# A mixture-of-experts and attention kernel: gathering results row by row instead of block by block

## The chip, the cores and the metric

The kernel runs on one core of a Trainium2 chip. Its engines work side by side, each on its own queue of instructions: TensorE (PE) multiplies matrices, VectorE (DVE) and ScalarE (ACT) work on rows, GpSimd (POOL) copies and issues indirect DMAs, and SyncE (SP) issues most of the plain DMAs. The metric is the device time of one execution in microseconds (us). Before the change it is 738.46 us, the median of three runs between 733.2 and 739.15.

## What is computed

The input is 4,096 tokens of 128 numbers (16 sequences of 256). Each passes a mixture-of-experts layer, an attention layer, and the same mixture-of-experts layer again, each added to the residual.

```python
x = x + 0.5 * _L0_ffn_ref(_layernorm(x, axis=-1), ...)
x = x + _L0_attn_ref(_layernorm(x, axis=-1), ...)
x = x + 0.5 * _L0_ffn_ref(_layernorm(x, axis=-1), ...)
```

The part that matters here is the expert layer. Every token chooses 4 of 32 experts, and its result is the sum of the four experts' outputs, each with the token's weight for that expert:

```python
vals, idx = jax.lax.top_k(gf, K)               # K = 4 of E = 32
w = jax.nn.softmax(vals, axis=-1)
combine = jnp.zeros((T, E)).at[jnp.arange(T)[:, None], idx].add(w)
h1 = jnp.einsum('th,efh->tef', tf, w1) + b1
hw = _swiglu(h1) * combine[:, :, None]
out = jnp.einsum('tef,ehf->th', hw, w2) + combine @ b2
return x + out.reshape(B, S, H)
```

The matmuls with data and weights are in float32; counts and masks are in bfloat16, where they are exact.

## The kernel before, in words

**Tiles.** The 4,096 tokens are 8 blocks of 512; four blocks form a group, so there are two groups (`n_grp` = 2, `GB` = 4). A block is held as 4 tiles of 128 tokens (`NJ` = 4). There are four expert runs: the first layer for groups 0 and 1 (`first[0]`, `first[1]`), and the last layer for groups 0 and 1 (`last[0]`, `last[1]`).

**To the experts.** `route` computes the gate, finds the top four experts of each token, the mask `m` (token chose expert), the weights `comb`, and each token's `rank` within its expert and tile. `dispatch` then finds where every expert's rows lie in the sorted order of the whole group. Tokens are sorted with matmuls against one-hot matrices (L677) into small blocks of five rows (`RB` = 5), all of one expert, and each tile's 128 such blocks are scattered with one indirect DMA (L596) into the DRAM buffer `xs[g]`. A block of five rows of 128 numbers is 2,560 B.

**The experts.** `experts` walks over 23 steps (`NQS`). In each it loads four tiles of 125 sorted rows, has POOL copy the four experts' first weights into a buffer (L717, five buffers), multiplies (L737), applies the activation on ACT and DVE (L741, L742, L747), multiplies again (L755), and writes the result rows to `ys[g]` in DRAM.

**Back from the experts.** `combined` undoes the sorting for one block of 512 tokens. For each tile of 128 tokens it gathers the same 128 small blocks with one indirect DMA (L786) from `ys[g]`, so four gathers per block. Then DVE builds a matrix `u` that holds, for each of the five rows of a small block, which token it belongs to and with which weight (L809, ten instructions per block), from two products `pa` and `pw` (L798 to L800); and PE multiplies it with the gathered rows (L816: 4 tiles x 5 rows, and each f32 matmul is two passes). The bias of the second expert weights is one more matmul per tile (L819), and the residual is added last (L822). The gathered tiles `gt` live in four buffers.

**What runs beside what.** `groups` strings the four expert runs together. Beside each run of experts, a generator of other work is advanced a few steps (`beside`) after every expert step:

- experts of `first[0]`, beside `enter(1)`: routing and dispatch of group 1
- experts of `first[1]`, beside `middle(0)`: for each block of group 0, `combined`, `attention` and `route` for the last layer, then `dispatch`
- experts of `last[0]`, beside `middle(1)`: the same for group 1
- experts of `last[1]`, beside `leave(0)`: `combined` of group 0, and the output is written
- after that, `leave(1)` alone: `combined` of group 1, and the output is written

`staggered` keeps up to three blocks of `middle` in flight, a new one after nine steps. The program text gives the order of priority; each engine's queue is laid out when the program is built, and an instruction that is ready early may be placed ahead, as the trace shows for small memsets. On the chip each queue then runs in its order.

Of the kernel before, what the change touches and what calls it, by code (L numbers as in the profile page):

```python
# [10 lines left out]
F32 = mybir.dt.float32  # L11
BF16 = mybir.dt.bfloat16
U32 = mybir.dt.uint32
I32 = mybir.dt.int32
AF = mybir.ActivationFunctionType
ALU = mybir.AluOpType
AX = mybir.AxisListType
# [5 lines left out]
P = 128  # L23
NJ = 4
TB = NJ * P
SEQ = 2
GB = 4
GJ = GB * NJ
NE = 32
TOPK = 4  # L30
# [6 lines left out]
RB = 5  # L37
# [7 lines left out]
NQ = NT // NJ  # L45
NQS = 23
NB = NT * BT
LIMIT = 7.0
ALPHA = 1.702
EPS = 1e-5  # L50
SILU_LIMIT = ALPHA * LIMIT / (1.0 + math.exp(-ALPHA * LIMIT))
NONE = -1.0e38
ROUND = 8388608.0


@with_exitstack
def kernel(
# [22 lines left out]
    nc = tc.nc  # L80
# [8 lines left out]
    const = ctx.enter_context(tc.tile_pool(name="const", bufs=1))  # L89
    wpool = ctx.enter_context(tc.tile_pool(name="weights", bufs=1))  # L90
    grp = ctx.enter_context(tc.tile_pool(name="grp", bufs=2))
# [108 lines left out]
    place_f = const.tile([P, FREE], F32, tag="place_f", name="place_f")  # L200
    nc.vector.tensor_scalar(place_f, step_f, self_f, None, ALU.add)

    ones = const.tile([P, P], BF16, tag="ones", name="ones")
    nc.gpsimd.memset(ones, 1.0)

# [76 lines left out]
    def bank(name):  # L282
        pool, tag = banks[0]
        banks.rotate(-1)
        return pool.tile([P, TB], F32, tag=tag, name=name)
# [115 lines left out]
    class Group:  # L401


        def __init__(self, g, name):
            self.g, self.name = g, name
            self.blocks = []
            self.n = grp.tile([P, GB], BF16, tag="n", name=f"n_{name}", bufs=3)
            self.row = grp.tile([P, 2, GJ], U32, tag="row", name=f"row_{name}", bufs=3)

        def held(self, b, tag, shape, dtype, bufs):  # L410
# [3 lines left out]
        def enter(self, b):  # L414
            self.blocks.append(Block())
            self.held(b, "tn", [P, NJ, P], F32, GB + 1)
            self.blocks[b].xr = dram.tile(
                [P, NJ * P], F32, tag=f"xr_{self.name}{b}", name=f"xr_{self.name}{b}"
            )

            self.held(b, "rank", [P, P], BF16, 2 * GB + 2)
            self.held(b, "combT", [P, P], F32, 2 * GB + 2)
            return self.blocks[b]

        def sort(self, b):
            self.held(b, "seg", [P, P], F32, 2 * GB + 2)
            self.held(b, "seg_b", [P, P], BF16, 2 * GB + 2)
            self.held(b, "off", [P, P], BF16, 2 * GB + 2)
            return self.blocks[b]

    def split(src, dtype, engine, tag, name, bufs=1):
# [12 lines left out]
    def route(st, src, b, co):  # L444

        name = f"{st.name}{b}"
        k = st.enter(b)
# [27 lines left out]
        for j in range(NJ):  # L475
            nc.vector.match_replace(left[:, j, :], v8[:, j, :], g[:, j, :], 2.0 * NONE)
        m = small.tile([P, NJ, NE], BF16, tag="m", name=f"m_{name}")
        nc.vector.tensor_tensor(m, left[:, :, 0:NE], g[:, :, 0:NE], ALU.not_equal)
        comb = small.tile([P, NJ, NE], F32, tag="comb", name=f"comb_{name}")
        nc.vector.tensor_tensor(  # L480
            comb, g[:, :, 0:NE], v8[:, :, 0:1].to_broadcast([P, NJ, NE]), ALU.subtract
        )
# [4 lines left out]
        nc.tensor.matmul(  # L487
            prank[:, 0 : 2 * P], m.rearrange("p j e -> p (j e)"),
            upto_self.rearrange("p c t -> p (c t)"), start=True, stop=True,
        )  # L490

        n = small.tile([P, 1], F32, tag="n32", name=f"n32_{name}")
# [33 lines left out]
    def dispatch(st, clear=False):  # L526
# [36 lines left out]
        for c in range(2):  # L563
# [6 lines left out]
        nc.vector.scalar_tensor_tensor(  # L570
            at, f[:, 0:1].to_broadcast([P, GB]), float(BT), at, ALU.mult, ALU.add
        )
        pick = small.tile([P, GB, 2 * NJ], F32, tag="pick", name=f"pick_{name}")
        nc.vector.tensor_copy(pick[:, :, NJ:], own.unsqueeze(1).to_broadcast([P, GB, NJ]))
        nc.vector.tensor_tensor(
# [81 lines left out]
        for b in range(GB):  # L657
# [8 lines left out]
            for t in range(NJ):  # L666
# [20 lines left out]
                    nxt = tables(b + 1)  # L687
                yield
        scattered[name] = sc

    def loaded(tab, q, engine, top):
        _, vals = nc.values_load_multi_w_load_instructions(
# [81 lines left out]
    def combined(st, b, tag):  # L774
# [45 lines left out]
                yield  # L820
        r = tmp.tile([P, NJ, P], F32, tag=tag, name=f"{tag}_{name}", bufs=3)
        nc.vector.tensor_tensor(r, pu, xr, ALU.add)  # L822
        yield r

    def logits(hT, w, name):
# [137 lines left out]
    def routes(g, gap, most):  # L963
        srcs = []
        for b in range(GB):
            if g * GB + b not in x_tiles:
                load_x(g * GB + b)
            srcs.append(x_tiles.pop(g * GB + b))
        co = coefficients(srcs, first[g].name)
        yield  # L970

        def block(b):
            yield from route(first[g], srcs[b], b, co[:, :, b * NJ : (b + 1) * NJ])

        yield from staggered((block(b) for b in range(GB)), gap, most)

    def enter(g, clear):
        first[g] = Group(g, f"{run_name}f{g}")
        yield from routes(g, 2, 2)
        yield from dispatch(first[g], clear)  # L980

    def middle(g):
        last[g] = Group(g, f"{run_name}l{g}")

        def block(b):
            for x1 in combined(first[g], b, "x1"):
                yield
            for x2 in attention(x1, f"{run_name}{g}{b}"):
                yield
            yield from route(last[g], x2, b, coefficients([x2], f"{last[g].name}{b}"))  # L990

        yield from staggered((block(b) for b in range(GB)), 9, 3, True)
        yield from dispatch(last[g])

    def leave(g):
        def block(b):
            for y in combined(last[g], b, "x1"):
                yield
            nc.sync.dma_start(
                out_blk[g * GB + b], y.rearrange("p (i s) h -> p i (s h)", i=SEQ)  # L1000
            )
            yield

        yield from staggered((block(b) for b in range(GB)), 3)
# [141 lines left out]
```

## Time and profile before

| | |
|---|---|
| median of three runs | 738.46 us |
| the profiled execution | 734.1 us |
| its span, first to last instruction | 732.0 us |
| busy: PE, PE weight loads | 620.1 us (85%), 574.3 us (78%) |
| busy: DVE, ACT, POOL | 483.1 us (66%), 379.5 us (52%), 284.5 us (39%) |
| mean granted TensorE clock | 0.938 |
| gathers L786, scatters L596 | 64 and 73 indirect DMAs |

Busy time is the time in which an engine executes; the rest is waiting. PE's busy time is not PE at its peak, since matmuls overlap. A share of the whole span is a mean over stages that have different limits, so the stages have to be read one by one. Instructions that only issue or wait are not counted as busy.

### The profile page before, as it was taken

Reading aid. Unit: us, or ns where it says so; the run is one execution under the profiler, and the core shown is the slowest. Engines: PE = TensorE matmul, PEld = TensorE weight load, DVE = VectorE, ACT = ScalarE, POOL = GpSimd, SP = SyncE. Lnnn points to the kernel's source line nnn. Section 1 sums busy time; section 2 is a strip of 40 time slices with the busy share of each in tenths; the row PEclk is TensorE's granted clock in tenths of the full one; section 3 lists DMA queues with packets and bytes.
Section 4 is the critical chain, followed back from the end, with each engine's and each line's share of the span. In section 5 each row is a group of like instructions: output and inputs, shape, how many; then the busy total and the mean of one; then the engine's idle time right before and its main releaser. Section 6 shows DMA issues by size and latency. Waiting matters only on the chain.

```text
span 732.0 us, 15990 instructions
## 1 busy us (share of the span) xinstructions
PE 620.1 (85%) x4897; PEld 574.3 (78%) x4897; DVE 483.1 (66%) x1823; ACT 379.5 (52%) x902; POOL 284.5 (39%) x567
## 2 busy tenths in 40 slices
PE   3677489979978988988997998988889789999595
PEld 1466389878978977977896887877789689999585
DVE  6863975855555688887774469888878535554443
ACT  2753376735543766864552455775655335445210
POOL 3023424467645422122365532402227645434242
PEclk9887779999999999998999999999999989999989
DMA  7999346477656435124355644513434667765463
GB/s 229 374 336 328 138 139 172 128 259 227 193 157 198 128 90 140 48 81 128 112 197 194 185 119 124 143 44 85 129 100 174 215 182 213 199 189 160 111 204 118
DMA packets 132695, 122.45 MB, mean 167 GB/s; under 512 B 9626, under 2 KB 118714, under 8 KB 132602
## 3 DMA queue, kind: packets, MB, share of 16 engines
q1 hardware_dynamic: 117658, 71.62, 34.6%
q0 software_dynamic: 10960, 44.90, 18.2%
q10 hardware_dynamic: 3984, 4.82, 1.8%
q8 instruction: 43, 0.70, 0.4%
q14 instruction: 50, 0.41, 0.2%
HBM read 57.78 MB, written 63.52 MB: 166 GB/s over the span
## 4 chain that ended last, share of the span: by engine, by line
PE 53%; DVE 21%; DMA 11%; ACT 7%; issue 6%; POOL 1%; another core or an unknown queue 0%; SPq 0%; POOLq 0%; ACTq 0%; DVEq 0%
PE ph_l L737 8%; PE ph_f L737 7%; PE p_l L677 4%; PE pu_f L816 4%; PE po_l L755 4%; PE po_f L755 4%; PE p_f L677 3%; PE pu_l L816 3%; DMA xs<-s_f,row_f 3%; PE pxT_l L723 2%; DMA gt_l<-ys,row_l 2%; DMA xq_l<-xs 1%; DMA w_sb<-in_w_dram 1%; PE pxT_f L723 1%; DVE lin_f L742 1%
## 5 line engine op out<-in xcount | busy, mean ns | idle before, releaser
L717 POOL COPY w_l<-w_sb 128x256 f32 x184 | 71.3, 416 | 124.4 <-PE ph_l L737 118.6
L717 POOL COPY w_f<-w_sb 128x256 f32 x184 | 70.3, 414 | 117.7 <-PE ph_f L737 116.2
L737 PE MATMUL ph_f<-xT_f,w_f 128*128 128x125 f32 x736 | 97.7, 281 | 1.4 <-DVE lin_f L742 1.1
L737 PE MATMUL ph_l<-xT_l,w_l 128*128 128x125 f32 x736 | 95.5, 279 | 0.1
L737 PEld LDWEIGHTS ph_f<-xT_f,w_f 128*128 128x128 f32 x736 | 90.9, 197 | 2.4 <-POOL w_f L717 1.4
L737 PEld LDWEIGHTS ph_l<-xT_l,w_l 128*128 128x128 f32 x736 | 89.6, 196 | 0.6 <-issue 0.3
L742 DVE TENSOR_SCALAR lin_l<-ph_l 128x250 f32<-128x250 f32 x92 | 37.8, 413 | 53.8 <-ACT a_l L741 53.3
L742 DVE TENSOR_SCALAR lin_f<-ph_f 128x250 f32<-128x250 f32 x92 | 37.5, 412 | 37.3 <-ACT a_f L741 36.2
L816 PE MATMUL pu_l<-gt_l,u_l 128*128 128x128 f32 x320 | 46.2, 290 | 11.5 <-DMA gt_l<-ys,row_l 7.5
L816 PEld LDWEIGHTS pu_l<-gt_l,u_l 128*128 128x128 f32 x320 | 42.7, 203 | 16.8 <-issue 9.8
L677 PE MATMUL p_f<-tn_f,o_f 128*128 128x128 f32 x320 | 46.3, 303 | 10.2 <-DVE rank_f L438 4.1
L677 PEld LDWEIGHTS p_f<-tn_f,o_f 128*128 128x128 f32 x320 | 43.1, 214 | 14.1 <-DVE rank_f L438 4.2
L816 PE MATMUL pu_f<-gt_f,u_f 128*128 128x128 f32 x320 | 45.7, 284 | 7.3 <-DMA gt_f<-ys,row_f 5.6
L755 PE MATMUL po_f<-w_sb,a_f 128*125 x368 | 49.9, 278 | 1.3 <-DVE a_f L747 0.9
L755 PE MATMUL po_l<-w_sb,a_l 128*125 x368 | 49.3, 277 | 1.4 <-DVE a_l L747 0.8
L741 ACT ACTIVATE a_l<-ph_l 128x250 f32<-128x250 f32 x92 | 34.7, 379 | 29.2 <-PE ph_l L737 25.1
L596 POOL DMA_INDIRECT xs<-s_f,row_f x32 | 31.3, 977 | 45.4 <-ACT s_f L682 23.4
L786 POOL DMA_INDIRECT gt_l<-ys,row_l x32 | 30.6, 958 | 44.2 <-PE pu_l L816 23.6
L816 PEld LDWEIGHTS pu_f<-gt_f,u_f 128*128 128x128 f32 x320 | 40.3, 194 | 9.3 <-DMA gt_f<-ys,row_f 5.2
L741 ACT ACTIVATE a_f<-ph_f 128x250 f32<-128x250 f32 x92 | 34.5, 381 | 23.8 <-PE ph_f L737 18.7
L755 PEld LDWEIGHTS po_f<-w_sb,a_f 128*125 128x125 f32 x368 | 45.0, 191 | 1.7 <-ACT yq_f L760 1.0
L755 PEld LDWEIGHTS po_l<-w_sb,a_l 128*125 128x125 f32 x368 | 44.9, 191 | 1.6 <-ACT yq_l L760 1.0
(339 smaller groups left out, 1456.9 us busy)
## 6 DMA issues: line engine op xcount, KB each, us to landing
xq_f<-xs SPq DMA_DIRECT2D x46, 224.0 KB
ys<-yq_f SPq DMA_DIRECT2D x46, 224.0 KB
xq_l<-xs SPq DMA_DIRECT2D x46, 224.0 KB
ys<-yq_l SPq DMA_DIRECT2D x46, 224.0 KB
xs<-zero SPq DMA_DIRECT2D x14, 500.0 KB
w_sb<-in_w_dram SPq DMA_DIRECT2D x4, 1024.0 KB
ys<-zero SPq DMA_DIRECT2D x2, 1250.0 KB
x<-in_x_dram SPq DMA_DIRECT2D x8, 256.0 KB
```

What stands on the lines that cost most here:

```text
L596: ins = nc.gpsimd.indirect_dma_start(out=xs[st.g][:, :], out_offset=bass.IndirectOffsetOnAxis(ap=index, axis=0), in_=rows.rearrange("p r h ...
L677: nc.tensor.matmul(p0[:, r, :] if r < 4 else p1[:, 0:P], o[:, r, :], k.tn[:, t, :], start=True, stop=True,)
L717: nc.gpsimd.tensor_copy(w[:, s, :], w_flat[:, bass.ds(at[2 * c + s], 2 * P)])
L723: nc.tensor.transpose(pt[:, t, 0:RT], xq[:, t, :], ident[:RT, :RT])
L737: nc.tensor.matmul(ph[:, part, s, 0:RT], w_q[c][:, s, part * P : (part + 1) * P], x_q[:, 2 * c + s, :], start=True, stop=True,)
L741: nc.scalar.activation(a[:, ts, :], ph[:, 0, :, 0:RT], AF.Silu, scale=ALPHA)
L742: nc.vector.tensor_scalar(lin[:, ts, :], ph[:, 1, :, 0:RT], LIMIT + 1.0, 1.0 - LIMIT, ALU.min, ALU.max,)
L755: nc.tensor.matmul(po[:RT, t, :], hT[:, t, :], w_flat[:, bass.ds(at[t] + 2 * P, P)], start=True, stop=True,)
L786: nc.gpsimd.indirect_dma_start(out=gt.rearrange("p r h -> p (r h)"), out_offset=None, in_=ys[st.g][:, :], in_offset=bass.IndirectOffsetOnA ...
L816: nc.tensor.matmul(pu[:, t, :], u[:, r, s, :], got[t][:, r, :], start=(r == 0), stop=False)
```

## The change

Three of the four combines now use a new function, `gathered`, in the place of `combined`; only `leave(1)`, the last phase, keeps `combined`. `gathered` reads each token's four result rows (512 B each) directly: 16 indirect DMAs per block, one for each tile and each of the four choices, and DVE multiplies each row with the token's weight and adds it, 16 instructions per block. The bias matmul and the residual stay. The matrix `u` and its products go.

For this the kernel has to know each token's four row numbers and weights in the order of tokens, not in the sorted order. `route` makes a second rank product, with tokens on the partitions, and keeps it with the mask in `rk` (a chosen expert is marked by the large constant `CHOSEN`); it keeps the weights in `cw`. The new generator `places` adds each expert's place in the sorted order, and takes the four largest entries of each token with DVE's maximum instruction; these are the row numbers `row_k`. A comparison with all 32 entries picks the weights `w_k`. `mixed` interleaves `places` with the other generators, every fourth step beside `enter(1)` and every sixth beside `middle`. The numbers of buffers of `rank`, `combT`, `seg`, `seg_b` and `off` shrink, since most of them aren't needed again later.

```diff
+I16 = mybir.dt.int16
+assert NB * RB < 16384
+CHOSEN = 16384.0
...
+    ones_f = const.tile([P, P], F32, tag="ones_f", name="ones_f")
+    nc.gpsimd.memset(ones_f, 1.0)
...
+            self.rk = grp.tile([P, GB, P], I16, tag="rk", name=f"rk_{name}")
+            self.cw = grp.tile([P, GB, NJ, NE], F32, tag="cw", name=f"cw_{name}")
...
-            self.held(b, "rank", [P, P], BF16, 2 * GB + 2)
-            self.held(b, "combT", [P, P], F32, 2 * GB + 2)
+            self.held(b, "rank", [P, P], BF16, GB + 1)
+            self.held(b, "combT", [P, P], F32, 2 * GB + 1)
...
-            self.held(b, "seg", [P, P], F32, 2 * GB + 2)
-            self.held(b, "seg_b", [P, P], BF16, 2 * GB + 2)
-            self.held(b, "off", [P, P], BF16, 2 * GB + 2)
+            self.held(b, "seg", [P, P], F32, GB + 1)
+            self.held(b, "seg_b", [P, P], BF16, GB + 1)
+            self.held(b, "off", [P, P], BF16, GB + 1)
...
-        comb = small.tile([P, NJ, NE], F32, tag="comb", name=f"comb_{name}")
+        comb = st.cw[:, b]
...
+        nc.tensor.matmul(
+            prank[:, 2 * P : 3 * P], upto_self[:, 0, :], m.rearrange("p j e -> p (j e)"),
+            start=True, stop=True,
+        )
+        nc.vector.scalar_tensor_tensor(
+            st.rk[:, b, :], prank[:, 2 * P : 3 * P], CHOSEN, m.rearrange("p j e -> p (j e)"),
+            ALU.add, ALU.mult,
         )
...
+        st.lo, st.at = lo, at
...
+    def places(st):
+
+        name = st.name
+        st.row_k = grp.tile([P, GJ, TOPK], U32, tag="row_k", name=f"row_k_{name}")
+        st.w_k = grp.tile([P, GJ, TOPK], F32, tag="w_k", name=f"w_k_{name}")
+
+        base = small.tile([P, GB], F32, tag="base", name=f"base_{name}")
+        nc.vector.tensor_tensor(base, st.at, st.lo, ALU.add)
+        nc.vector.tensor_scalar(base, base, float(RB), -1.0 - CHOSEN, ALU.mult, ALU.add)
+        for b in range(GB):
+            js = slice(b * NJ, (b + 1) * NJ)
+            work = tmp.tile([P, RB, 2, P], F32, tag="u", name=f"work_{name}{b}", bufs=2)
+            diag, d = work[:, 0, 0, :], work[:, 0, 1, :]
+            found = work[:, 1:3].rearrange("p a c (k e) -> p (a c) k e", k=TOPK)
+            nc.vector.tensor_scalar(diag, ident, base[:, b : b + 1], None, ALU.mult)
+            pd = bank(f"pd_{name}{b}")
+            nc.tensor.matmul(pd[:, 0:P], ones_f, diag, start=True, stop=True)
+            nc.vector.tensor_tensor(d, pd[:, 0:P], st.rk[:, b, :], ALU.add)
+            d = d.rearrange("p (j e) -> p j e", j=NJ)
+            d8 = small.tile([P, NJ, 8], F32, tag="d8", name=f"d8_{name}{b}")
+            for j in range(NJ):
+                nc.vector.max(d8[:, j, :], d[:, j, :])
+            nc.vector.tensor_copy(st.row_k[:, js, :], d8[:, :, 0:TOPK])
+            nc.vector.tensor_tensor(
+                found, d.unsqueeze(2).to_broadcast([P, NJ, TOPK, NE]),
+                d8[:, :, 0:TOPK].unsqueeze(3).to_broadcast([P, NJ, TOPK, NE]), ALU.is_equal,
+            )
+            nc.vector.tensor_tensor(
+                found, found, st.cw[:, b].unsqueeze(2).to_broadcast([P, NJ, TOPK, NE]), ALU.mult
+            )
+            nc.vector.tensor_reduce(st.w_k[:, js, :], found, AX.X, ALU.add)
+            yield
+
+    def mixed(main, other, every):
+
+        for i, _ in enumerate(main):
+            if i % every == every - 1:
+                next(other, None)
+            yield
+        yield from other
...
+    def gathered(st, b, tag):
+
+        name = f"{st.name}{b}"
+        k = st.blocks[b]
+        rows = ys[st.g].rearrange("n (r h) -> (n r) h", r=RB)
+        xr = tmp.tile([P, NJ, P], F32, tag="xr", name=f"xri_{name}", bufs=3)
+        nc.sync.dma_start(xr.rearrange("p j h -> p (j h)"), k.xr)
+        got = []
+
+        def get():
+            j = b * NJ + len(got)
+            gt = tmp.tile([P, RB, P], F32, tag="gt", name=f"gt_{st.name}{j}", bufs=4)
+            for i in range(TOPK):
+                nc.gpsimd.indirect_dma_start(
+                    out=gt[:, i, :],
+                    out_offset=None,
+                    in_=rows,
+                    in_offset=bass.IndirectOffsetOnAxis(ap=st.row_k[:, j, i : i + 1], axis=0),
+                )
+            got.append(gt)
+
+        get()
+        get()
+        comb4 = split(k.combT, F32, nc.scalar, "comb4", name, 2)
+        yield
+        pu = bank(f"pu_{name}").rearrange("p (j h) -> p j h", j=NJ)
+        for t in range(NJ):
+            nc.tensor.matmul(pu[:, t, :], comb4[:, t, :], b2_sb, start=True, stop=True)
+        r = tmp.tile([P, NJ, P], F32, tag=tag, name=f"{tag}_{name}", bufs=3)
+        nc.vector.tensor_tensor(r, pu, xr, ALU.add)
+        get()
+        yield
+        for t in range(NJ):
+            for i in range(TOPK):
+                nc.vector.scalar_tensor_tensor(
+                    r[:, t, :], got[t][:, i, :], st.w_k[:, b * NJ + t, i : i + 1], r[:, t, :],
+                    ALU.mult, ALU.add,
+                )
+            if len(got) < NJ:
+                get()
+            yield
+        yield r
...
     def enter(g, clear):
         first[g] = Group(g, f"{run_name}f{g}")
-        yield from routes(g, 2, 2)
-        yield from dispatch(first[g], clear)
+
+        def chain():
+            yield from routes(g, 2, 2)
+            yield from dispatch(first[g], clear)
+
+        yield from mixed(chain(), places(first[0]) if g else iter(()), 4)
 
     def middle(g):
...
-            for x1 in combined(first[g], b, "x1"):
+            for x1 in gathered(first[g], b, "x1"):
                 yield
...
-        yield from staggered((block(b) for b in range(GB)), 9, 3, True)
-        yield from dispatch(last[g])
+        def chain():
+            yield from staggered((block(b) for b in range(GB)), 9, 3, True)
+            yield from dispatch(last[g])
+
+        yield from mixed(chain(), places(last[0] if g else first[1]), 6)
 
     def leave(g):
         def block(b):
-            for y in combined(last[g], b, "x1"):
+            for y in (combined if g else gathered)(last[g], b, "x1"):
                 yield
```

More of the change, by code (lines that the diff above doesn't have):

```diff
@@ L822, in combined @@
         nc.vector.tensor_tensor(r, pu, xr, ALU.add)
+        yield r
[33 more added lines that the diff above has]
+                    ALU.mult, ALU.add,
+                )
+            if len(got) < NJ:
+                get()
+            yield
         yield r
```

## The prediction

> **What bounds the kernel now.** I read four views: busy time by stage, the groups of instructions, the timeline of POOL, and the spread of single lines. First the stages. The cuts are my own, at the first expert matmul (L737) of each of the four expert runs: start-up, experts of group 0 beside the routing of group 1 (A), experts of group 1 beside `middle(0)` (B), experts of group 0 again beside `middle(1)` (C), experts of group 1 again beside `leave(0)` (D), and `leave(1)` alone. Columns: stretch, length, then busy time of PE, weight loads, VectorE (DVE), ScalarE, GpSimd (POOL).
>
> ```profile
> 0.00:99.00 99.00, 61.44 (x338) 47.02 (x339) 67.50 (x346) 44.41 (x116) 26.58 (x71) 0.81 0.81 268
> 99.00:211.00 112.00, 103.61 (x895) 99.98 (x894) 69.72 (x211) 66.67 (x154) 60.68 (x125) 0.97 0.61 187
> 211.00:407.00 196.00, 169.07 (x1352) 158.20 (x1351) 140.07 (x561) 109.20 (x257) 74.66 (x138) 0.95 0.47 138
> 407.00:593.00 186.00, 163.25 (x1309) 151.56 (x1309) 139.46 (x558) 106.41 (x255) 68.26 (x126) 0.96 0.45 134
> 593.00:686.00 93.00, 92.15 (x803) 90.62 (x802) 47.88 (x100) 47.39 (x108) 39.18 (x91) 0.98 0.62 173
> 686.00:732.00 46.00, 30.56 (x210) 26.90 (x209) 18.44 (x47) 5.38 (x13) 15.15 (x16) 0.90 0.52 156
> ```
>
> D is bound by PE (92 of 93 us). B and C are bound by no one engine: PE 86 to 88%, DVE 71 to 75%, in a chain of gather, combine, attention and routing. POOL looks free everywhere. Next, what the change touches (busy and mean ns, then idle time before):
>
> ```profile
> L816 PE MATMUL pu_f<-gt_f,u_f 128*128 128x128 f32 x320 | 45.7, 284 | 7.3 <-DMA gt_f<-ys,row_f 5.6 <-DVE u_f L809 1.5 <-issue 0.2
> L786 POOL DMA_INDIRECT gt_f<-ys,row_f x32 | 31.7, 989 | 33.1 <-PE pu_f L816 13.3 <-PE pu_f L819 12.0 <-issue 3.8
> L809 DVE SCALAR_TENSOR_TENSOR u_f<-pa_f,wb_f 128x256 f32<-128x256 f32 x80 | 29.3, 412 | 7.6 <-ACT wb_f L802 7.6
> L636 DVE SCALAR_TENSOR_TENSOR seg_l<-iota_f,hi_l,seg_l 128x128 f32<-128x128 f32 x8 | 3.1, 392 | 0.0
> L883 DVE TENSOR_TENSOR v<-pv,zs 128x512 f32<-128x512 f32 x8 | 5.5, 683 | 1.0 <-PE pv L878 1.0
> L717 POOL COPY w_l<-w_sb 128x256 f32 x184 | 71.3, 416 | 124.4 <-PE ph_l L737 118.6 <-PE pt_l L292 3.4 <-PE ph_f L737 0.7
> ```
>
> POOL's idle time is mostly a wait for a free expert-weight buffer (118.6 us before L717), so POOL runs as far ahead as five buffers let it: true slack. But a gather costs more than its 0.95 us. The timeline of POOL, where gathers follow each other at the start of the last stage, and one run of weight copies in B:
>
> ```profile
> 690.34 0.97 POOL L786 DMA_INDIRECT gt_l<-ys,row_l  x1 [12.74 <-DMA ys<-yq_l]
> 691.62 0.94 POOL L786 DMA_INDIRECT gt_l<-ys,row_l  x1 [0.30 <-issue]
> 692.87 0.95 POOL L786 DMA_INDIRECT gt_l<-ys,row_l  x1 [0.30 <-issue]
> 694.12 0.95 POOL L786 DMA_INDIRECT gt_l<-ys,row_l  x1 [0.30 <-DMA gt_l<-ys,row_l]
> ...
> 220.06 1.42 POOL L717 COPY w_f<-w_sb 128x256 f32 x4
> ```
>
> Start to start is 1.25 us: 0.95 busy and 0.30 of issue that no busy share counts. The four weight copies of one expert step take 1.42 us.
>
> **The change, part by part.** Three of the four combines (first groups 0 and 1, last group 0: 12 of 16 blocks) change.
>
> *Removed from PE, per block:* 40 passes of L816, ten of them 1.12 us start to start, 4.5 us; L798 and L799, 0.21 us each; L800, 0.86 us. Together 5.8 us, 23 us in each of B, C and D, 70 us in all. The bias matmul L819 stays. Added on PE: one bf16 matmul in each `route` and one small f32 matmul per block of `places`, by the row of L487 (0.28 us) under 0.3 us each, under 9 us in all, in B and C where PE is relieved; I count 0.
>
> *Added on POOL, per block:* 16 gathers of 128 rows of 512 B for 4 of 2,560 B: 12 more, 12 x 1.25 = 15 us, 60 us for each of B, C, D and 180 us in all. The trace shows only 2,560 B rows, each DMA with 128 indices. Low end: if the cost goes with bytes, a fifth, 0.19 + 0.30 = 0.5 us, and 16 of them cost 8 us against 5 now. High end: the slowest gather of L786, 1.44 + 0.30 = 1.7 us. I take 1.25, as the row count stays 128. Here a rule speaks for the low end: the Trainium skill (DMA: Bandwidth & Descriptors, Anatomy of one DMA) calls descriptor generation small and variable, and gives most of a DMA's fixed 2 us to the write receipt. With POOL charged only the issue gap, 0.3 us, the additions would be 3.6 us per block and hidden, and the sum the first rival's. The row has POOL busy for 0.95 us on every gather, so I go by the row.
>
> *On DVE, per block:* the ten L809 leave (five take 1.75 us: 0.34 each, 3.4 us) and L438 (0.69). Added: 16 operations of 128 columns, two SBUF inputs and a scalar from memory. Nearest is L636, 0.34 to 0.39 us; four in a row depend on each other, so I take the whole duration, 0.36, 5.8 us. Net +1.7 us. `places`, per block: a diagonal (L635, 0.3), an addition out of PSUM (L499, 0.28), four maxima (L473, 0.18 each, overlapping to 0.46 in the timeline), a cast (L652, 0.17), compare, product and reduction over 512 columns (L883 and L831, 0.68 each, 2.05): 3.3 us, 13 us per group, in A, B and C. One product per `route`, 0.28 us. So A +14, B and C +21 each, D +7, start-up +1.
>
> Now the rule against the change: the Trainium skill (SBUF — State Buffer, Who interferes with whom) says that a DVE instruction with two SBUF inputs and a GpSimd instruction that reads SBUF exclude each other for the whole instruction. The removed L809 had one input in PSUM; its replacement has both in SBUF, beside L717. The rows (min/median/max ns):
>
> ```profile
> L809 DVE SCALAR_TENSOR_TENSOR u_f<-pa_f,wb_f x80: 390/411/425, 211.9 to 487.5; 128x256 f32<-128x256 f32 x80
> L747 DVE SCALAR_TENSOR_TENSOR a_l<-a_l,lin_l x46: 642/678/1587, 411.3 to 684.3; 128x500 f32<-128x500 f32 x46
> L717 POOL COPY w_l<-w_sb x184: 386/401/887, 365.1 to 677.2; 128x256 f32 x184
> ```
>
> L809 never stretches; L747, with two SBUF inputs, stretches now and then. Its mean (710) is 5% over its median: by the row, 0.3 us per block. By the rule, if each of the 16 met a copy, 16 x 0.4 = 6.4 us per block, 26 us per stage, and the sum would be the third rival's. I take the row and keep the other for the range.
>
> **Where it lands.** *Start-up +1* (`rk` in four `route`s). *A +3*: 14 us of DVE in a stage with DVE at 62%, mostly covered by PE-bound expert steps of 3.1 us; without that cover, 14.
>
> *B +14.* The combines end (L822) at 228.7, 252.1, 280.6 and 308.3, so a block takes 23 to 28 us. POOL now needs 16 x 1.25 = 20 plus 1.42 for each of some four expert steps, 26 us. Its first gather can't start before 214.7, when the last expert rows have landed; block 0 then ends near 240 instead of 229, and at 26 to 27 us apiece the fourth near 320, 12 late. Queued behind those gathers on POOL are the weight copies of the next step, and behind them PE; four gather buffers are one block ahead at most, so they can't be pulled forward. In DVE's queue the sums wait for gathers with the experts' L742 and L747 behind them. DVE rises to 161 of 196; I add 5 for it and take back 3 for the relieved PE. *C +8*: block 0's gathers fit in the gap at the change of stage (gathers run from 389.9, experts start at 407), so some 10 us of the first delay falls away, half of it lost again on POOL's queue, where 16 gathers stand among the last scatters.
>
> *D +12.* PE falls to 69 us. POOL: 23 steps x 1.42 = 33, and with block 0 again gathered in the gap, 48 x 1.25 = 60: 93, as long as the whole stage was. The steps of `leave` fill only the first 16 of 23 expert steps; 12 of those beside the 48 gathers take 60 + 17 = 77, and the 9 or so others 3.1 each, 28: 105.
>
> Last stage 0: its code is the same. Sum +38. The profiled run took 734.1 us, 2.1 beyond its span, and makes 772. The median shown, 738.46, is 4.4 above it, between runs of 733.2 and 739.15; I add half and say 774.
>
> **The rivals.**
> *Cheap gathers, faster (0.14).* A row gather costs POOL 0.5 us. Then 23 us of PE leaves D nearly whole (-18) and B and C win about 8 each: 738 - 34 + 4 for `places` = 708. Against it: the 0.95 us shows hardly any spread. It turns where a gather's pitch is about 0.9 us, 14 us per block.
> *Everything covered (0.11).* The order of POOL's work lets gathers fill its slack, and the relieved PE pays for DVE: 731 to 746. For it: 124.4 us idle before L717. Against it: D's 93 us on POOL without one wait.
> *DVE and POOL wait for each other (0.18).* Copies and two-input sums block each other and gathers take 1.7 us: POOL's 16 gathers cost 27 + 6 per block, B +35, C +25, D +30: 830 us.
> That the change does less than it says is nearly excluded: the row indices go into real DMAs.
>
> **How the numbers follow.** My likeliest case, 750 to 800, has 0.57. The range runs from 726, which leaves most of the cheap case out, to 830, the mutual case's middle: some 0.2 outside. Within 1%, which is about what this measurement can tell from no change, lies the covered case. Faster 0.14, same 0.11, slower 0.75.
>
> **What would show it.** POOL's timeline in D: gathers back to back at 1.25 us, little waiting for PE, PE's share down to about 70%. In B, the first L822's successor near 240. The groups: 192 gathers of about 0.95 us; PE less by 70 us. I am wrong if the gathers' pitch is under 0.9 us, or if D is no longer than 93 us.

## The result and the profile after

The changed kernel takes 858.24 us (857.41 to 860.96, four runs) against 737.52 us before: a ratio of 1.165, 95% interval 1.160 to 1.171. The prediction was 774, with a range to 830. The direction was right, the forecast rise (35 us) less than a third of the measured one (121 us). The profiled execution took 857.99 us, with a span of 856.2.

First the stages of the changed kernel, cut at the same places as before (stretch, length, then busy time of PE, weight loads, DVE, ACT, POOL, the granted PE clock, the DMA share and GB/s):

```profile
99.00:212.00 113.00, 104.81 (x917) 101.39 (x917) 78.72 (x266) 69.85 (x161) 64.23 (x126) 0.98 0.62 188
212.00:453.00 241.00, 157.04 (x1153) 145.60 (x1152) 155.41 (x636) 101.37 (x253) 121.93 (x184) 0.81 0.34 101
453.00:699.00 246.00, 154.32 (x1158) 145.23 (x1157) 152.43 (x615) 105.82 (x258) 127.70 (x189) 0.81 0.34 102
699.00:811.00 112.00, 88.46 (x650) 85.26 (x649) 54.66 (x119) 42.97 (x95) 75.68 (x126) 0.87 0.49 137
811.00:856.00 45.00, 29.56 (x204) 26.52 (x204) 17.78 (x46) 4.79 (x12) 15.13 (x16) 0.90 0.51 155
```

A and the last stage are as they were. B goes from 196 to 241 us, C from 186 to 246, D from 93 to 112. In B and C no engine comes near its limit: PE falls from 86-88% to 63-65%, DVE is at 62-64%, POOL at about 51%. So the 105 us lost in B and C are waiting. PE's clock goes with it, from 0.95 to 0.81.

Now the groups that answer to those of before (line, engine, form, count, then busy us and mean ns, then idle time before them and what ended it):

```profile
L897 POOL DMA_INDIRECT gt_f<-ys,row_k_f x128 | 124.6, 974 | 54.1 <-issue 35.0 <-DVE v_l L481 7.2 <-DVE cw_l L488 6.1
L796 PEld LDWEIGHTS ph_f<-xT_f,w_f 128*128 128x128 f32 x736 | 96.7, 208 | 42.6 <-issue 32.6 <-POOL w_f L776 9.9
L776 POOL COPY w_f<-w_sb 128x256 f32 x184 | 74.4, 437 | 113.2 <-PE ph_f L796 109.2 <-remote 1.6 <-PE po_f L814 0.9
L918 DVE SCALAR_TENSOR_TENSOR x_f<-gt_f,w_k_f,x_f 128x128 f32<-128x128 f32 x128 | 42.6, 357 | 26.0 <-DMA gt_f<-ys,row_k_f 20.8 <-issue 4.9
L801 DVE TENSOR_SCALAR lin_l<-ph_l 128x250 f32<-128x250 f32 x92 | 37.4, 412 | 64.8 <-ACT a_l L800 57.9 <-issue 6.8
```

L897 are the row gathers, L776 the weight copies (L717 before), L796 the first expert matmul (L737), L918 the new sums, L801 the experts' `lin` (L742). The single instructions cost what the prediction took for them: a gather 0.97 us, a sum 0.357. And POOL still sits 113 us idle before the copies L776 of the first layer, nearly all of it (109) waiting for PE to free a weight buffer. An engine can have slack in one stretch and be what everybody waits for in the next; a sum over the whole run doesn't show that.

The timeline of one such stretch, from the first block of B (start, duration, engine, line, tiles, count, in brackets the idle time before it and what ended it):

```profile
237.97 3.62 PE L796 MATMUL ph_f<-xT_f,w_f 128*128 128x125 f32 x16
239.29 0.97 POOL L897 DMA_INDIRECT gt_f<-ys,row_k_f  x1 [0.16 <-issue]
...
241.39 1.90 PE L814 MATMUL po_f<-w_sb,a_f 128*125 x8
...
258.05 0.94 POOL L897 DMA_INDIRECT gt_f<-ys,row_k_f  x1 [0.30 <-issue]
258.99 1.42 POOL L776 COPY w_f<-w_sb 128x256 f32 x4
259.01 0.38 ACT L800 ACTIVATE a_f<-ph_f 128x250 f32<-128x250 f32 x1 [21.98 <-remote]
259.43 0.42 DVE L801 TENSOR_SCALAR lin_f<-ph_f 128x250 f32<-128x250 f32 x1 [17.65 <-issue]
...
259.99 2.04 PE L796 MATMUL ph_f<-xT_f,w_f 128*128 128x125 f32 x8 [16.70 <-issue]
```

From 239.3 to 259.0 POOL issues 16 gathers without a break, 1.25 us apart. Behind them stand the next expert step's weight copies (258.99). PE stops at 243.3 and starts again at 260.0. Two things are in this picture. The copies come late, which explains PE's wait. And ACT's `a` at 259.01 waited 22 us for a matmul that PE began at about 238: a late update (a semaphore update is the signal by which an engine tells another that its result is ready), not a late copy. The experiments had to tell these two apart, and each from a third: sums in DVE's queue that wait for gathers.

### The profile page after: what moved, and what is told of

Read it like the earlier page. It is cut to its first block, busy times and chain, and to the rows that moved or that the text cites. A ratio compares the mean times of both kernels' runs of the same rounds, so it can differ in the third digit from the quotient of the medians.

```text
span 856.2 us, 15468 instructions
## 1 busy us (share of the span) xinstructions
PE 594.6 (69%) x4407; PEld 549.8 (64%) x4409; DVE 525.6 (61%) x2025; ACT 367.3 (43%) x888; POOL 431.3 (50%) x712
## 5 line engine op out<-in xcount | busy, mean ns | idle before, releaser
L897 POOL DMA_INDIRECT gt_f<-ys,row_k_f x128 | 124.6, 974 | 54.1 <-issue 35.0
L796 PE MATMUL ph_l<-xT_l,w_l 128*128 128x125 f32 x736 | 110.9, 307 | 49.9 <-DVE lin_l L801 19.5
L796 PEld LDWEIGHTS ph_l<-xT_l,w_l 128*128 128x128 f32 x736 | 103.4, 221 | 54.1 <-issue 41.5
L796 PE MATMUL ph_f<-xT_f,w_f 128*128 128x125 f32 x736 | 104.8, 294 | 39.5 <-issue 16.7
L776 POOL COPY w_f<-w_sb 128x256 f32 x184 | 74.4, 437 | 113.2 <-PE ph_f L796 109.2
L796 PEld LDWEIGHTS ph_f<-xT_f,w_f 128*128 128x128 f32 x736 | 96.7, 208 | 42.6 <-issue 32.6
L776 POOL COPY w_l<-w_sb 128x256 f32 x184 | 73.3, 432 | 99.4 <-PE ph_l L796 75.8
L801 DVE TENSOR_SCALAR lin_l<-ph_l 128x250 f32<-128x250 f32 x92 | 37.4, 412 | 64.8 <-ACT a_l L800 57.9
L897 POOL DMA_INDIRECT gt_l<-ys,row_k_l x64 | 62.4, 974 | 16.6 <-issue 15.2
L801 DVE TENSOR_SCALAR lin_f<-ph_f 128x250 f32<-128x250 f32 x92 | 37.3, 410 | 52.7 <-ACT a_f L800 34.0
L814 PE MATMUL po_l<-w_sb,a_l 128*125 x368 | 57.2, 299 | 12.8 <-issue 9.9
L814 PEld LDWEIGHTS po_l<-w_sb,a_l 128*125 128x125 f32 x368 | 51.0, 211 | 14.1 <-issue 10.9
L782 PE MATMUL pxT_l<-ident,xq_l 125*128 125x125 f32 x184 | 33.1, 306 | 37.8 <-ACT xT_l L784 21.1
L918 DVE SCALAR_TENSOR_TENSOR x_f<-gt_f,w_k_f,x_f 128x128 f32<-128x128 f32 x128 | 42.6, 357 | 26.0 <-DMA gt_f<-ys,row_k_f 20.8
L782 PEld LDWEIGHTS pxT_l<-ident,xq_l 125*128 125x128 f32 x184 | 25.0, 160 | 39.7 <-ACT xT_l L784 22.1
```

What stands on the lines that cost most here:

```text
L776: nc.gpsimd.tensor_copy(w[:, s, :], w_flat[:, bass.ds(at[2 * c + s], 2 * P)])
L782: nc.tensor.transpose(pt[:, t, 0:RT], xq[:, t, :], ident[:RT, :RT])
L796: nc.tensor.matmul(ph[:, part, s, 0:RT], w_q[c][:, s, part * P : (part + 1) * P], x_q[:, 2 * c + s, :], start=True, stop=True,)
L801: nc.vector.tensor_scalar(lin[:, ts, :], ph[:, 1, :, 0:RT], LIMIT + 1.0, 1.0 - LIMIT, ALU.min, ALU.max,)
L814: nc.tensor.matmul(po[:RT, t, :], hT[:, t, :], w_flat[:, bass.ds(at[t] + 2 * P, P)], start=True, stop=True,)
L897: nc.gpsimd.indirect_dma_start(out=gt[:, i, :], out_offset=None, in_=rows, in_offset=bass.IndirectOffsetOnAxis(ap=st.row_k[:, j, i : i + 1 ...
```

## The experiments

Three theories: **Q**, runs of gathers stand in POOL's queue ahead of weight copies; **C**, runs of gathers hold up PE's completions themselves; **V**, the sums wait in DVE's queue with the experts' DVE work behind them. All results in one table. A, B and C run from the first expert matmul of their expert run to that of the next; D ends with the last store to `ys` (D before is 94 by this cut). Where the copies are on ACT in A, the first expert matmul comes at 90 to 94 us in place of 97 to 101, so A starts earlier there. "Group" is explained under the repetition below; the rows of group I may be compared with each other, and so may those of group II.

| kernel | us | before, beside it | A | B | C | D | last | group |
|---|---|---|---|---|---|---|---|---|
| before, first trace | | 737.5 | 112 | 196 | 186 | 94 | 45 | II |
| after, first trace | 858.2 | 737.5 | 113 | 240 | 246 | 112 | 45 | II |
| e9 after, again | 863.5 | 739.3 | 113 | 241 | 250 | 111 | 45 | II |
| e10 row numbers worked out twice | 867.8 | 739.3 | 126 | 244 | 221 | 126 | 44 | II |
| g2 copies on ACT, gathers spread | 884.0 | 740.0 | 126 | 254 | 237 | 126 | 44 | II |
| f1 after | 806.6 | 732.5 | 107 | 220 | 207 | 125 | 45 | I |
| e1 / f2 copies on ACT | 757.6 / 757.2 | 730.3 / 732.5 | 119 / 117 | 194 / 197 | 190 / 190 | 114 / 114 | 45 / 46 | I |
| e2 / f3 gathers spread, two per step | 797.3 / 801.6 | 730.3 / 732.5 | 108 / 109 | 226 / 232 | 209 / 212 | 105 / 105 | 45 / 45 | I |
| e3 gathers spread, four per three steps | 796.7 | 730.3 | 108 | 224 | 206 | 110 | 45 | I |
| e4 before, with unused gathers | 821.0 | 730.3 | 107 | 228 | 210 | 130 | 44 | I |
| g1 the same, copies on ACT | 764.8 | 729.6 | 115 | 208 | 195 | 111 | 45 | I |
| e5 before, copies on ACT | 732.7 | 732.0 | 114 | 196 | 186 | 95 | 45 | I |
| e6 / f4 no sums in D | 799.2 / 798.3 | 732.0 / 732.5 | 110 / 110 | 221 / 219 | 206 / 211 | 116 / 114 | 44 / 45 | I |
| e7 no sums in D, copies on ACT | 722.8 | 732.0 | 119 | 194 | 190 | 79 | 46 | I |
| e8 mix | 761.0 | 732.0 | 109 | 204 | 202 | 106 | 44 | I |

**First: copies moved, gathers spread, gathers alone.** e1 moves the weight copies to ACT:

```diff
-            at = loaded(st.at_w, q, POOL, (NE - 1) * EW)
+            at = loaded(st.at_w, q, ACT, (NE - 1) * EW)
...
-                    nc.gpsimd.tensor_copy(
+                    nc.scalar.copy(
```

> The kernel after, with the experts' weight copies moved from POOL to ACT; POOL keeps only gathers and scatters. Before: 737.5 us, stages B, C, D 196, 186, 93; after: 858.2 us, 240, 246, 110. Theory Q (the unbroken runs of 16 gathers stand in POOL's queue ahead of the weight copies, and PE starves for weights): the 44 and 60 us lost in B and C shrink to about 15 each, D is near 95, total about 770, though ACT gets some 368 copies of 0.4 us. Theory C (a run of back-to-back gathers holds up PE's semaphore updates, wherever the copies are): PE and ACT still stand still during the runs, total 840 or more. Theory V (sums in DVE's queue wait for gathers, with the experts' DVE work behind them): hardly better, 840 or more, DVE's waits for gather DMAs unchanged at about 45 us.

e2 breaks `get` up, so that a `yield` stands after every two gathers, and a tile's sums come one tile later; e3 has four gathers and then three `yield`s:

```diff
+                    if i % 2 == 2 - 1:
+                        if i == TOPK - 1:
+                            got.append(gt)
+                        for _ in range(1):
+                            yield
```

> The kernel after, with the gathers issued two per step of the generator in the place of eight, four and four: in B the queue then holds runs of mostly 4 to 6 gathers between weight copies, not 16. Theory Q: B and C fall by 20 to 30 us each, total about 800. Theory C: the updates are held for shorter times, total also about 800. Theory V: the number of gathers and sums is the same and the sums come no earlier: 850 or more.

> As the run before, with four gathers and then three steps: runs of 4 to 8 gathers, and every block takes some five steps longer. Theories Q and C: between 790 and 830; if the longer way of a block decides, no better than 850. Theory V: 850 or more.

e4 puts 12 gathers that nobody reads into `combined`, in three groups of four:

```diff
+        def more():
+            for t in range(NJ if extra else 0):
+                gd = tmp.tile([P, 16], F32, tag="gd", name="gd", bufs=4)
+                nc.gpsimd.indirect_dma_start(
+                    out=gd, out_offset=None, in_=rows,
+                    in_offset=bass.IndirectOffsetOnAxis(
+                        ap=st.row[:, 0, b * NJ + t : b * NJ + t + 1], axis=0
+                    ),
+                )
```

> The kernel before, with 12 more gathers per block in the same three combines (128 rows of 64 B each, into a buffer that nobody reads), so POOL has the changed kernel's number of indirect DMAs while DVE and PE do the work of the kernel before. Runs are 8, 4, 4 in B's first blocks and up to 14 later. Theory Q: 180 us more on POOL, part of it hidden; B and C +25 to +40 each, D +15, total 800 to 830. Theory C: the same, with PE's updates late by over 100 us in the sum. Theory V: nobody waits for these gathers, at most 755.

The ratios to before are 1.037 (1.029 to 1.046) for e1, 1.093 for e2 and e3, and 1.127 (1.116 to 1.138) for e4. e4 is the plainest. It has neither the sums nor the new DVE work, PE does all that it did before, and it still loses 91 us. Its groups say to whom; L737 of the kernel before stands first:

```profile
L737 PE MATMUL ph_f<-xT_f,w_f 128*128 128x125 f32 x736 | 97.7, 281 | 1.4 <-DVE lin_f L742 1.1
L737 PE MATMUL ph_l<-xT_l,w_l 128*128 128x125 f32 x736 | 95.5, 279 | 0.1
...
L737 PE MATMUL ph_l<-xT_l,w_l 128*128 128x125 f32 x736 | 102.2, 289 | 45.2 <-POOL w_l L717 45.0
L737 PE MATMUL ph_f<-xT_f,w_f 128*128 128x125 f32 x736 | 100.0, 284 | 29.6 <-POOL w_f L717 27.9 <-DVE lin_f L742 1.4
L782 POOL DMA_INDIRECT gd<-ys,row_f x96 | 92.2, 960 | 27.0 <-issue 24.8 <-DMA gd<-ys,row_f 1.2 <-PE pxT_f L723 0.3
```

PE waits 73 us for the copies L717; before, it stood idle for 1.5 us ahead of L737 in all. The unused gathers fetch 64 B per row and take 0.96 us each, much as those of 512 (0.97) and of 2,560 B (0.99). V alone, which gave at most 755 here, is out as the main cause. e1 takes the loss in B and C away almost entirely (194 and 190). The same trace, however, has D at 114, where Q gave about 95.

**Second: a control, and D.** e5 moves the copies in the kernel before; e6 and e7 leave the sums of `leave(0)` out (the range of the inner loop becomes 0 for `last[0]`), with the copies on POOL and on ACT:

> Control for the run with the copies on ACT: the kernel before with its weight copies on ACT. If the place of the copies matters only because runs of 16 gathers stand ahead of them, this is no gain: A 7 us longer (ACT gets 92 copies per stage), B and C within 5 us of 196 and 186, total 735 to 755. If ACT is simply the better place, B and C fall by 10 us or more and the total is under 725.

> The kernel after, with the 64 sums per group on DVE left out in the first leaving phase only (stage D; the four gathered rows aren't added for group 0, its output lacks them; all gathers stay). Theory Q (POOL's queue holds the weight copies back in D too): D stays at 105 to 112. Theory V (in D the sums wait for gathers with the experts' DVE work behind them): D falls to 97 or less. A, B, C as after (113, 240, 246).

> The kernel after with the copies on ACT and, as in the run before, the sums of stage D left out. With the copies on ACT, D was 114. Theory V: with neither copies behind gathers nor experts behind sums, D falls to 80 to 92. If it stays above 105, what lengthens D is ACT (the copies) or the gathers' transfers themselves.

e5 is 0.9997 of before (0.997 to 1.003): ACT isn't a better place for the copies as such, it is only a place without gathers. In D, the waits of e1 (engine, line, what it waited for: us in total, times, longest) name the second queue:

```profile
DVE x_l L919 <- DMA gt_l<-ys,row_k_l: 31.0, 28, 2.7
...
PE ph_l L797 <- DVE lin_l L802: 25.1, 8, 12.4
```

and those of e6 the first:

```profile
PE ph_l L796 <- POOL w_l L776: 27.5, 11, 5.7
```

With the copies on ACT, the sums (L919 there) wait 31 us for gathers, and `lin` stands behind them. With the sums out but the copies on POOL, PE waits for copies. Either one alone holds D at 114 to 116 (with both, it is 125 in f1 below); only with both gone does D fall, to 79, so the gathers' transfers, which e7 has all of, are not what lengthens D. There PE is the bound again, as this row of e7's stages shows:

```profile
596.00:675.00 79.00, 75.46 (x651) 73.66 (x649) 36.09 (x71) 65.24 (x181) 53.78 (x55) 0.98 0.74 197
```

e8 was meant to use this: copies on POOL in A and on ACT elsewhere, and in `leave(0)` four gathers per three steps with the sums two tiles behind.

> A version meant to beat both: copies on POOL in A and on ACT in B, C and D; in D the gathers are spread evenly over the steps (four per three steps) and each tile's sums stand two tiles behind its gathers, so they should not wait. From Q and V together: A 112, B and C about 194 and 190 as with the copies on ACT, D 80 to 90, total 720 to 735 against 737.5. If D's length comes from ACT or from the transfers, D stays above 105 and the total above 745.

It missed: 1.040 of before (1.036 to 1.044). D was 106; the sums still waited 24 us for gathers: 64 gathers at 1.25 us are 80 us of POOL. With four buffers the sums could stand at most one tile later still, which was not tried. A is 10 us shorter than in e7, but its first matmul comes 4 us later, and B gives the 10 us back (A and B together 313 in both). C is 202, 12 us above e7; why B and C didn't keep to 194 and 190 stays open. No version here computes everything and beats the kernel before; e7, without the sums of one stage, takes 722.8 us, 0.989 of before (0.984 to 0.995). That is about the most that hiding them could bring.

**A repetition that changed the reading.** e6 has the instructions of the changed kernel in the same order on every engine in B and C, but took 221 and 206 us there, not 240 and 246. So the changed kernel was run again, and beside it e10, in which the body of `places` runs twice.

> The changed kernel itself once more, nothing edited, because the run without sums in D has the same order of instructions on every engine in B and C, and yet took 221 and 206 us there against 240 and 246 in the first run of the changed kernel. If that first run is the kernel's own time, about 858 us comes again, with B and C near 240 and 246 and PE's semaphore updates late by some 187 us in the sum; then something other than the order of instructions (where code or data lie) costs 59 us. If the first run was disturbed, or its chip was another case, about 795 to 800 us, B 221, C 206, D 110 to 116, no late updates.

> The kernel after, with the work of the new generator for row numbers and weights done twice (the second time over the first, same values): 3.3 us more DVE work per block, 13 us more in each of A, B and C. The prediction held that most of it is covered: A +3, B +5, C under +5, so 5 to 15 us over the changed kernel run beside it. If DVE's queue is on the path in B and C, +25 to +40. If covered fully, under 4.

858 came again, as 863.5. The difference goes with the chip. The chips of these runs fall into two groups. In group II (the first pair of runs, whose chip isn't recorded; chip 7 with e9 and e10; chip 5 with g2) PE's semaphore updates reach the waiting engines late, and 6 to 9% of them are missing in the trace. In group I (chip 10 with e1 to e4, 12 with e5 to e8, 3 with f1 to f4, 15 with g1) they are there and on time, but for three in g1. Each chip was used at one time only, so chip and time can't be told apart. Counted from the traces, as updates more than 1.2 us after the last modelled end of a matmul that makes one, without those at the end of the program:

```
kernel            late updates   sum, us   longest   beside a run of 3+ indirect DMAs
before (II)             8           19        3.0     8
after (II)             43          181       18.9    40
e9 (II)                47          240       35.7    44
e10 (II)               43          247       37.0    41
g2 (II)                57          298       12.2    57
f1, after (I)           0            0        -       -
e1 to e8, f2 to f4      0            0        -       -
g1 (I)                  3            8        3.0     1
```

"Beside" means during such a run or up to 5 us after it; such stretches are 389 of the changed kernel's 856 us, so 40 of 43 is no accident. The sums count updates that are late together several times; they are not time lost. f1 has such runs for 296 us, and none late: the runs alone don't make updates late. So e1 to e4 had been compared with a kernel measured on another kind of chip. The next four kernels ran on one chip.

> The changed kernel, nothing edited, beside three of the earlier variants on one chip. If late PE updates are a matter of the chip: either about 800 us (B 221, C 206, D 116, none late), or 858 to 864 with late updates in the other three too. If they belong to this kernel alone: 858 to 864 with the other three at 757, 797 and 799 as before.

> Copies on ACT, once more beside the changed kernel. 757 us where the changed kernel is 800: moving the copies is worth 43 us. Where the changed kernel is 860, theory Q says that with nothing behind the gathers late updates cost little: at most 775; theory C says 810 or more.

> Gathers two per step, once more beside the changed kernel. Where the changed kernel is 800, it is 797: the length of the runs is nothing and only the amount of POOL's work ahead of the copies counts. Where the changed kernel is 860: about 800 if long runs cause the late updates, 850 if not.

> The changed kernel without the sums of stage D (group 0's output lacks the experts' part), once more beside the changed kernel. Same B and C as the changed kernel on the same chip, whichever they are; D at 110 to 116 in both, which would show that with the copies on POOL the sums cost D nothing.

It was a chip of group I. The changed kernel takes 806.6 us there, 1.100 of before (1.093 to 1.107); copies on ACT 757.2; spread gathers 801.6; no sums in D 798.3. B and C of f1, and below them those of f2 with the copies on ACT:

```profile
207.00:427.00 220.00, 152.64 (x1148) 141.93 (x1147) 153.50 (x636) 101.28 (x252) 122.59 (x184) 0.85 0.38 111
427.00:634.00 207.00, 150.75 (x1158) 141.50 (x1157) 149.34 (x604) 105.81 (x258) 116.08 (x177) 0.88 0.39 116
...
210.00:406.00 196.00, 149.00 (x1141) 138.34 (x1140) 148.10 (x636) 125.13 (x341) 87.85 (x96) 0.89 0.42 124
407.00:596.00 189.00, 147.15 (x1154) 139.64 (x1153) 141.68 (x604) 130.64 (x346) 80.22 (x82) 0.89 0.43 127
```

D is 125 in f1 and 114 in f4, not 110 to 116 in both: with the copies on POOL the sums cost D 11 us. Against f1, spreading is worth 5 us, not the 60 that it seemed to be worth: B is even 12 us longer, though its runs fall from 16 gathers to mostly 4 to 6, and D is 20 shorter. So in B the length of a run isn't what costs, by this run; but the edit also gives each block more steps and later sums, so the two aren't parted. The timeline of f1 shows Q without any late update:

```profile
240.02 0.59 PE L782 MATMUL pxT_f<-ident,xq_f 125*128 125x125 f32 x4
...
241.67 0.84 PE L297 MATMUL ph<-ident,h 128*128 128x128 f32 x3 [1.06 <-DVE h L960]
...
251.48 0.94 POOL L897 DMA_INDIRECT gt_f<-ys,row_k_f  x1 [0.30 <-issue]
252.72 0.94 POOL L897 DMA_INDIRECT gt_f<-ys,row_k_f  x1 [0.30 <-issue]
253.66 2.44 POOL L776 COPY w_f<-w_sb 128x256 f32 x7
254.13 0.79 PE L796 MATMUL ph_f<-xT_f,w_f 128*128 128x125 f32 x2 [11.62 <-POOL w_f L776]
...
254.71 0.42 PE L297 MATMUL ph<-ident,h 128*128 128x128 f32 x1
...
255.17 0.58 ACT L967 COPY hT<-ph 128x512 f32<-128x512 f32 x1 [13.84 <-PE ph L297]
```

Now the wait is named: PE stands 11.6 us for `w_f`. And it costs more than the expert step. PE had done three of the four transposes L297 of the attention; the fourth stands in PE's queue behind the expert matmul that waits for weights. So ACT's `hT`, and with it the chain of the block, waits 13.8 us for POOL as well.

**Two last ones.** g1 is e4 with the copies on ACT, g2 is e2 with the copies on ACT.

> The kernel before with 12 unused row gathers per block in three combines and the weight copies on ACT. Theory Q: 821 us with the copies on POOL falls to 733 to 745 (the kernel before with copies on ACT is equal to the kernel before), B and C within 5 us of 196 and 186. If the gathers hold something up by themselves (transfers, late PE updates): 770 or more, wherever the copies are.

> The kernel after with both: copies on ACT, and gathers issued two per step. With the copies on ACT alone 757 (D 114), with spread gathers alone 797 to 802 (D 105). Theory V: the sums of D stand later in DVE's queue and wait less, D 90 to 100, B and C as with the copies on ACT or a few us longer (each block takes some five steps longer), total 740 to 752. If it is 757 or more, spreading moves no wait that matters. On a chip with late PE updates: at most 775 if they cost only what is queued behind the gathers, 810 or more if not.

g1 takes 764.8 us: of e4's loss of 91 us, 56 go with the copies and 35 stay. Part of the latter are gathers behind gathers: PE now waits for `gt`, the rows that are used, which stand behind those that aren't (in B, 11.2 us in three waits). Both figures of the expectation were wrong; Q has a second part, that POOL delays its own block. g2 fell on a chip of group II and took 884 us, with B 254 and C 237 though nothing but gathers and scatters is left on POOL. With one of its two edits, e1 and f3 took 757 and 802 on group I. Both edits together weren't run on group I. But the 57 late updates of g2, all of them beside gathers, can't come from copies behind the gathers: on such a chip what C describes is seen without them. The timeline of g2 shows it:

```profile
275.26 1.92 PE L815 MATMUL po_f<-w_sb,a_f 128*125 x8
...
280.20 0.95 POOL L906 DMA_INDIRECT gt_f<-ys,row_k_f  x1 [0.30 <-issue]
283.09 0.38 ACT L801 ACTIVATE a_f<-ph_f 128x250 f32<-128x250 f32 x1 [3.84 <-remote]
```

PE's last matmul in the records ends at 277.2, the last gather of the run at 281.1, and seven updates of PE arrive together between 283.0 and 283.4.

## Why the prediction was right and wrong

**Right.** The pitch of 1.25 us, and its independence of the bytes: rows of 64, 512 and 2,560 B take POOL the same, so the low price, which the quoted page stood for, is excluded. A sum costs 0.357 us in B and C, predicted 0.36 (0.416 in D, with one of 2.5 us). The rule of two SBUF inputs was weighed and kept for the range, rightly; in the changed kernel (min/median/max ns):

```profile
L918 DVE SCALAR_TENSOR_TENSOR x_f<-gt_f,w_k_f,x_f x128: 322/347/704, 219.7 to 585.3; 128x128 f32<-128x128 f32 x128
L918 DVE SCALAR_TENSOR_TENSOR x_l<-gt_l,w_k_l,x_l x64: 336/352/2535, 673.2 to 778.6; 128x128 f32<-128x128 f32 x64
L806 DVE SCALAR_TENSOR_TENSOR a_l<-a_l,lin_l x46: 616/678/1122, 477.7 to 808.1; 128x500 f32<-128x500 f32 x46
L776 POOL COPY w_l<-w_sb x184: 386/401/1293, 409.3 to 801.0; 128x256 f32 x184
```

The medians of L806 and L776 are where they were. But the sums do stretch where they meet a copy: 34 of the 192 overlap one in time and take 486 ns in mean, the other 158 take 353 (32 with 569 and 160 with 347 in f1). That is 4.5 us in the whole kernel, where the rule, charged to all, gave 26 us per stage: what was small is how often they meet. Block 0 of B ends at 239.9, predicted near 240 (234.1 in f1). The last stage is unchanged, A is 1 us longer (predicted 3). The cost of `places` is covered about as said: done twice it costs 4 us in all (867.8 against 863.5), less than the runs of either kernel differ (13 and 8 us), though A alone takes all 13 us of it and C came out 29 us shorter: one stage of one trace is not to be overread.

**Wrong: B +14 and C +8.** They were +45 and +60 on the chip of the result, and +24 and +21 on a chip of group I; here the sum of +38 fell short. The step that failed is the one that turns POOL's 26 us per block into a delay. It let the blocks follow each other every 26 to 27 us and charged only the lateness of the fourth block. In fact blocks 1 to 3 of B end at 282.8, 327.7 and 360.8, 33 to 45 us apart (in f1 at 268.9, 305.6 and 331.9, 26 to 37 apart). The prediction did name both queues, "in DVE's queue the sums wait for gathers with the experts' L742 and L747 behind them", and on POOL "the weight copies of the next step, and behind them PE", but gave neither a price beyond that cadence. With POOL busy for 20 us at a stretch and two steps of weights in five buffers, PE has some 8 us of work left and then stands for about 12; the block's attention stands with it in PE's queue, so the next gathers are late too. Copies on ACT, which remove that, bring B and C to 194-197 and 190, nearly their lengths before, while in the kernel before the same move changes nothing (e5). That shows it for group I.

**The rest of it, on group II.** Another 20 us in B and 39 in C. Late updates go with it: 30 of the 43 lie in B and C, and each engine's order of instructions is that of f1. That they cause all of it is argued, not shown, and why these chips have them stays open. Nothing in the sum stood for it. The trace of before had a sign: its only late updates before the end of the program, eight of them, 1.3 to 3.0 us, lie behind runs of indirect DMAs, of which it had 66 us in all. The changed kernel has 268 us.

**Too large by its own measure:** the 70 us taken off PE. PE's busy time fell by 25, from 620.1 to 594.6. Up to 9 us are the added matmuls, which the prediction counted as 0. The rest goes with a longer mean of the matmuls that stayed, while the granted clock fell between the stalls: L796 takes 277 ns in A (clock 0.98) and 310 and 308 in B and C (0.81), L737 took 278 to 282. In D, PE is busy for 79% (forecast: about 70%). There, where PE was the bound, the relief shows once the queues are out of the way: 79 us in e7, which lacks the sums, against 94. In B and C it bought next to nothing: with the copies on ACT they are 194 to 197 and 190, not 23 us shorter than before.

**D +12 was near by luck.** It came out as +18 on the chip of the result and +31 on group I (125). It was built from POOL's time alone, with a slip: 12 steps beside gathers and 9 others make 21 of the 23, and with 11 others the sum would have been 111, next to the 112 of the first trace. But POOL's time isn't all that holds D: in f1 the sums wait 40 us there for gathers, and PE 27 us for `lin` behind them. The sum for D had no term for that, and either of the two queues alone holds it at 114 to 116. A second slip costs nothing: the "ends" of the combines are the starts of their last instruction, 0.7 us early.

**The rivals.** Cheap gathers and a covered change were both excluded by the runs. The third rival's 830 lies nearer the result than the forecast, but not by its mechanism: gathers take 0.97 us, not 1.7, and copies and sums meet too seldom. The range that ended there was too narrow for what is left: a price for a queue standing still.

## What to carry to other kernels

Before adding work to an engine that looks idle, list what stands behind it in that engine's queue, how many buffers its consumers have, and for how long they last; slack that is a wait for a free buffer is used up by a single stretch of work longer than those buffers. Then ask the same of the engine that consumes what was added: removing one of two queues that each hold the same stage gained 11 of the 46 us here, until the other was gone too. And measure variants on the same chip as what they are compared with.

## What was not expected of the hardware

On group II, PE's semaphore updates came up to 37 us late, 43 to 57 times per execution of the kernels with row gathers, nearly all of them during or just after unbroken runs of POOL's indirect DMAs, and often several within 0.4 us. By the same measure ACT's and POOL's were never late, and DVE's 1 to 5 times, by at most 3.9 us. But the traces of this group lack updates of every engine: in the first trace of the changed kernel 8% of PE's, 14% of DVE's, 13% of ACT's and 10% of POOL's, most of them beside such runs too, so what happened to those isn't known. On four chips of group I none of this, or next to none, was seen. The changed kernel took 807 us on the one of these on which it ran, in place of 858 to 864 (before: 730 to 732 on the four, in place of 738 to 740). Since the ends of matmuls are modelled, it stays open whether the matmuls themselves or only their updates are late, and why these chips differ. Shorter runs weren't really tried on such a chip: in g2, with nothing but gathers and scatters on POOL, runs of up to 28 remained. And the cost of an indirect DMA on POOL, 0.94 to 0.95 us (median) and 0.30 between two, was the same for rows of 64, 512 and 2,560 B.
